# Layer 0's routing: the engine that clears the table of shares

## The chip, the cores and the metric

The kernel runs on one core of a Trainium2 chip. A core has five engines, each with its own queue of instructions, which it takes strictly in order: TensorE (PE; its weight loads are listed apart as PEld), VectorE (DVE), ScalarE (ACT), GpSimd (POOL) and SyncE (SP, which here only starts transfers). They wait for each other through semaphores. The metric is the device time of one execution in microseconds (us); lower is better.

## The reference

A stack of four layers on 4 rows of 512 tokens with 128 channels, float32. Each layer adds half a feed-forward part, then attention, then half the same feed-forward part again, always on a normalized copy of `x`. The change lies in the feed-forward part of layer 0, a mixture of eight experts of which each token uses two, and a ninth, shared expert:

```
x = x + 0.5 * _L0_ffn_ref(_layernorm(x), ...)
x = x + _L0_attn_ref(_layernorm(x), ...)
x = x + 0.5 * _L0_ffn_ref(_layernorm(x), ...)
...
def _L0_ffn_ref(x, gate_w, gate_b, w1, b1, w3, b3, w2, b2, sw1, ...):
    scores = softmax(xt @ gate_w.T)
    _, idx = top_k(scores + gate_b, 2)
    weights = take_along_axis(scores, idx)
    comb = (weights[..., None] * one_hot(idx, 8)).sum(1)
    for each expert:  acc += comb[:, e] * (swiglu((xt @ w1 + b1) * (xt @ w3 + b3)) @ w2 + b2)
    shared = swiglu((xt @ sw1 + sb1) * (xt @ sw3 + sb3)) @ sw2 + sb2
    return acc + shared
```

`comb` is the table of shares: per token, the weight of each of the eight experts, zero for those not chosen.

## The kernel before

The kernel is one long program. Its first stage, some 90 us, is the routing of layer 0's first feed-forward part (`by_expert`, `route`). `route(b)` handles one of the four rows, its 512 tokens as 4 tiles of 128: normalize (`layernorm_parts`; the power step L322 is on GpSimd), transpose (L342), gate matmul (L517), exponentials and the ranking of the experts on VectorE (L365 to L370, `taken` L528, `sofar` L533), two small matmuls that count tokens ahead of each other (L540, L541), the destination rows `irows` (L544 to L549), and then eight indirect transfers from GpSimd's queue (L586) that scatter the row's tokens into `sorted_x`, expert by expert.

Beside it the table `comb` is made: a tile of 128 partitions by 4 x 32 floats, of which columns 0 to 7 are the experts' shares and column 8 is 0.5 for the shared expert; the rest has to be zero, since the whole tile is transposed by TensorE (L568) and multiplied with the experts' biases (L573, added to `x` by L353). L551 clears it, `weigh` writes column 8 (L554) and the shares (L555), then computes `share` (L557 to L560). `comb` comes from a pool with two buffers, so the clear for row b+2 has to wait until row b's table has been transposed (L568) and read (L557).

While the rows are routed, TensorE and the others do two more things: `fold` (L635, L636) subtracts weights from each other, 16 matmuls of 128x512, and `common` (L606 to L626) computes the shared expert for every row: L606 fills one of three `big` accumulator tiles with two matmuls, ScalarE takes one half (L608), VectorE the other (L611), so that the tile comes free. `plan` (L646 to L698) then turns the counts into a list of tiles, `iwho`. From about 90 us on, `tiles` fetches sorted tiles (`xs`, L740, on SyncE's queue; each fetch waits for all 32 scatters), transposes them (L751) and runs the experts (L761 and after).

Then comes layer 0's attention (`l0_attn_quick`, scores L1203, values L1217, the reciprocal of the sums L1229, its use L1237 and L1239, output L1246). There TensorE's order is written out by hand, and in its gaps rows 0 to 2 are routed a second time, for the second feed-forward part; so `route` runs eight times in all, and L551 with it.

Except for TensorE in attention and a last stretch that has an order of its own, the order in each engine's queue is not that of the source: a scheduler puts each engine's instructions in an order it thinks they can run in. Moving one instruction to another engine therefore also changes the order of others around it.

The file also holds a second, safer version of the whole program behind a condition; it does not run with these inputs.

Of the kernel before, what the change touches and what calls it, by code (L numbers as in the profile page):

```python
# [270 lines left out]
def program(ctx: ExitStack, tc: tile.TileContext, a: dict, out: bass.AP, worst):  # L271

    nc = tc.nc
# [191 lines left out]
    def by_expert(w, rooms, key):  # L465
# [33 lines left out]
        def route(b, work, rows_pool=None, slow=False):  # L499
# [48 lines left out]
            nc.vector.tensor_reduce(rows[:, b], mine, AX.X, ALU.add)  # L548
            nc.vector.tensor_copy(irows[:, b], rows[:, b])  # L549
            comb = tiny.tile([P, NT, 32], F32, tag="comb", name="comb", bufs=2)  # L550
            nc.gpsimd.memset(comb, 0.0)  # L551

            def weigh():
                nc.vector.memset(comb[:, :, NE], 0.5)  # L554
# [405 lines left out]
        def fetched(b, work):  # L960
# [19 lines left out]
            while got:  # L980
                yield DVE(0.35, at=got[0][3])
                add()

        return SimpleNamespace(route=route, common=common, fold=fold, plan=plan, tiles=tiles, back=back, ready=ready, fetched=fetched, tiled=tiled, needs=needs)

    def chain(*parts):
# [1841 lines left out]
```

## Time and profile before

| | us |
|---|---|
| median of three runs | 1305.28 |
| the three runs | 1305.28, 1298.9, 1309.57 |
| the profiled execution | 1288.94 |
| its span, first to last instruction | 1287.2 |
| L551, the eight clears: one takes | 0.204 to 0.236 |
| starts of the first and last of them | 0.7, 450.8 |
| VectorE waiting at L554 for L551, 3 times | 12.0 in all |
| an indirect transfer L586 on GpSimd, 64 of them | 1.108 mean |

In the profile a line of the timeline has the start, the length, the engine, the source line, the operation, what it writes and reads with shapes, how many records were merged, and in brackets how long the engine stood idle before it and what ended that. A float32 matmul appears as two records. "issue" is idle time in which the engine waited for nothing that the profile shows. A chain of waits is followed back from the last instruction: at each step to what released it. The granted clock is the share of its full clock that TensorE was given.

### The profile page before, as it was taken

Reading aid. Unit: us, or ns where it says so; the run is one execution under the profiler, and the core shown is the slowest. Engines: PE = TensorE matmul, PEld = TensorE weight load, DVE = VectorE, ACT = ScalarE, POOL = GpSimd, SP = SyncE. Lnnn points to the kernel's source line nnn. Section 1 sums busy time; section 2 is a strip of 40 time slices with the busy share of each in tenths; the row PEclk is TensorE's granted clock in tenths of the full one; section 3 lists DMA queues with packets and bytes.
Section 4 is the critical chain, followed back from the end, with each engine's and each line's share of the span. In section 5 each row is a group of like instructions: output and inputs, shape, how many; then the busy total and the mean of one; then the engine's idle time right before and its main releaser. Section 6 shows DMA issues by size and latency. Waiting matters only on the chain.

```text
span 1287.2 us, 20162 instructions
## 1 busy us (share of the span) xinstructions
PE 1174.3 (91%) x6954; PEld 630.3 (49%) x6954; DVE 895.4 (70%) x2328; ACT 700.6 (54%) x1015; POOL 328.1 (25%) x320
## 2 busy tenths in 40 slices
PE   5899989999999999988899949989999999999995
PEld 3455644334335335355455548765596544543333
DVE  5597767888988988769667945868735873365233
ACT  2435535653644544533345523556757777787872
POOL 4340223032220400202123554533224121041000
PEclk9899989999999999989899987899999999999998
DMA  8123311121110210201321140000011000000000
GB/s 308 33 73 90 89 60 52 66 76 38 57 66 33 80 48 37 67 1 40 106 73 44 36 133 23 26 12 23 26 50 38 5 18 18 17 25 1 9 9 11
DMA packets 63490, 65.00 MB, mean 50 GB/s; under 512 B 11538, under 2 KB 53908, under 8 KB 62868
## 3 DMA queue, kind: packets, MB, share of 16 engines
q1 hardware_dynamic: 57236, 51.04, 11.9%
q0 software_dynamic: 6144, 12.60, 3.3%
q8 instruction: 58, 0.95, 0.3%
q14 instruction: 52, 0.42, 0.1%
HBM read 29.13 MB, written 17.69 MB: 36 GB/s over the span
## 4 chain that ended last, share of the span: by engine, by line
PE 63%; DVE 21%; issue 5%; DMA 3%; ACT 3%; POOL 2%; SPq 1%; DVEq 0%; POOLq 0%; ACTq 0%
PE big L1956 8%; PE one L1998 8%; PE big L1203 5%; PE one L1217 5%; PE big L761 4%; PE one L1541 3%; PE big L883 3%; PE one L1246 2%; PE big L606 2%; DVE sums L1212 2%; PE big L1153 2%; PE one L2475 1%; PE one L2019 1%; PE big L635 1%; PE one L794 1%
## 5 line engine op out<-in xcount | busy, mean ns | idle before, releaser
L1972 ACT ACTIVATE pT<-big 128x1024 f32<-128x1024 f32 (+1 forms) x224 | 205.0, 963 | 52.7 <-PE big L1956 44.3
L1204 ACT ACTIVATE pT<-big 128x1024 f32<-128x1024 f32 x128 | 125.7, 1034 | 55.7 <-PE big L1203 53.0
L1203 PE MATMUL big<-qk 64*128 64x512 f32 x512 | 127.5, 609 | 6.8 <-DVE U L1239 6.8
L1956 PE MATMUL big<-qkq,qkk 32*128 32x512 f32 (+3 forms) x1024 | 130.9, 555 | 0.1
L1217 PE MATMUL one<-pT,V 128*64 128x512 f32 x512 | 116.9, 598 | 0.0
L1998 PE MATMUL one<-pT,V 128*32 128x512 f32 (+3 forms) x1024 | 111.5, 522 | 2.5 <-DVE through L2029 0.8
L1504 POOL TENSOR_TENSOR rs<-rs,root 128x4 f32<-128x4 f32 x35 | 37.1, 1059 | 226.8 <-DVE rs L1502 183.5
L586 POOL DMA_INDIRECT sorted_x<-xn,irows x64 | 70.9, 1108 | 69.8 <-DVE share L558 22.4
L1212 DVE TENSOR_TENSOR sums<-sums,pT 128x1024 f32<-128x1024 f32 x64 | 78.1, 1220 | 5.7 <-ACT pT L1204 1.1
L1203 PEld LDWEIGHTS big<-qk 64*128 64x128 f32 x512 | 46.6, 187 | 69.5 <-issue 40.9
L1956 PEld LDWEIGHTS big<-qkq,qkk 32*128 32x128 f32 x1024 | 49.2, 184 | 61.8 <-issue 40.8
L883 PE MATMUL big<-w_w,xsT 128*128 x156 | 76.2, 620 | 2.5 <-ACT xsT L1355 2.4
L761 PE MATMUL big<-w_w,xsT 128*128 x156 | 73.5, 595 | 0.4 <-issue 0.4
L1217 PEld LDWEIGHTS one<-pT,V 128*64 128x64 f32 x512 | 33.9, 136 | 77.1 <-issue 72.4
L842 POOL DMA_INDIRECT yg<-sorted_y,ito x32 | 40.1, 1254 | 123.0 <-DMA sorted_y<-ys 61.8
L1294 ACT COPY U<-one 128x512 f32<-128x512 f32 x32 | 18.8, 587 | 94.7 <-PE one L1217 92.6
L606 PE MATMUL big<-xnT,w_w 128*128 128x512 f32 x128 | 61.4, 616 | 6.9 <-DVE u L611 5.8
L353 DVE TENSOR_TENSOR x<-x,one 128x512 f32<-128x512 f32 x31 | 21.2, 684 | 57.2 <-PE one L1541 33.1
L1984 DVE TENSOR_TENSOR pT<-pT,w_c_tri 128x256 f32<-128x256 f32 (+1 forms) x96 | 52.4, 563 | 2.5 <-ACT pT L1972 2.2
L608 ACT ACTIVATE t<-big,w_bs 128x512 f32<-128x512 f32 x32 | 21.7, 685 | 56.5 <-PE big L606 30.9
L322 POOL TENSOR_TENSOR rs<-rs,root 128x4 f32<-128x4 f32 x16 | 20.7, 1298 | 118.7 <-DVE rs L321 118.6
L1998 PEld LDWEIGHTS one<-pT,V 128*32 128x32 f32 x1024 | 23.9, 108 | 54.6 <-issue 37.9
(448 smaller groups left out, 2418.4 us busy)
## 6 DMA issues: line engine op xcount, KB each, us to landing
other<-qk SPq DMA_DIRECT2D x64, 256.0 KB, 2.2
xs<-sorted_x SPq DMA_DIRECT2D x78, 64.0 KB, 1.8
sorted_y<-ys SPq DMA_DIRECT2D x38, 128.0 KB, 1.8
w_w<-in_w SPq DMA_DIRECT2D x2, 2048.0 KB
w_l_w<-in_l_w SPq DMA_DIRECT2D x8, 256.0 KB, 3.2
w_l_w<-in_l_w SPq DMA_DIRECT2D x1, 2048.0 KB, 8.4
X<-row_x SPq DMA_DIRECT2D x8, 256.0 KB, 3.5
row_y<-y SPq DMA_DIRECT2D x8, 256.0 KB, 2.3
```

The lines of the kernel that those rows point to most:

```text
L586: apart(nc.gpsimd.indirect_dma_start(out=sorted_x[:, :], out_offset=bass.IndirectOffsetOnAxis(ap=irows[:, b, j, t : t + 1], axis=0), in_=x ...
L606: nc.tensor.matmul(pa[:, m, :], lhsT=w["w13"][:, NE, m, odd, c * P : (c + 1) * P], rhs=xTs[b], start=True, stop=True)
L761: nc.tensor.matmul(pa[:, k, :], lhsT=st[u]["xT"][:, k * P : (k + 1) * P], rhs=w["w13"][:, bass.ds(st[u]["e"][k], 1), m].rearrange("p o a b ...
L883: nc.tensor.matmul(pa[:, k, :], lhsT=xT[:, k * P : (k + 1) * P], rhs=w["w13"][:, bass.ds(e[k], 1), m].rearrange("p o a b -> p (o a b)"), s ...
L1203: nc.tensor.matmul(sT[:, u, :], lhsT=k[r, t * P : (t + 1) * P], rhs=q[r, :], start=True, stop=True)
L1204: nc.scalar.activation(pT[:, :, t % 2, :], sT, AF.Exp, scale=scale)
L1212: nc.vector.tensor_tensor(s, s, pT[:, :, m, :], ALU.add)
L1217: nc.tensor.matmul(po[r, :], lhsT=V[:, t, :], rhs=pT[:, u, t % 2, :], start=(t == 0), stop=(t == NT - 1), tile_position=(0, 64 * u))
L1956: nc.tensor.matmul(sT[j // 2][:, j % 2, c : c + n], lhsT=keys[k][r, t * P : (t + 1) * P], rhs=turns[k, g][r, S - n :], start=True, stop=True)
L1972: nc.scalar.activation(p[:, :, :n], sets[i][h][:, :, :n], AF.Exp, scale=scale)
L1984: nc.vector.tensor_tensor(d, d, w["c_tri"].unsqueeze(1).unsqueeze(1).to_broadcast([P, 2, len(parts), P]), ALU.min)
L1998: nc.tensor.matmul(po[32 * j : 32 * j + 32, S - n :], lhsT=V[k % 2][:, t, NJ * g + j, :], rhs=us[i][j // 2][:, j % 2, c : c + n], start=(t ...
```

## The change

L551 is issued on VectorE instead of GpSimd. Nothing else is edited.

```diff
@@ -548,7 +548,7 @@
             nc.vector.tensor_reduce(rows[:, b], mine, AX.X, ALU.add)
             nc.vector.tensor_copy(irows[:, b], rows[:, b])
             comb = tiny.tile([P, NT, 32], F32, tag="comb", name="comb", bufs=2)
-            nc.gpsimd.memset(comb, 0.0)
+            nc.vector.memset(comb, 0.0)
 
             def weigh():
                 nc.vector.memset(comb[:, :, NE], 0.5)
```

In the order that the scheduler makes of it, the eight clears are gone from GpSimd's queue. On VectorE two stand at the very start, two right behind `share` of rows 0 and 1 (L558), two beside the first tiles, and one each behind the routing of rows 0 and 1 in attention, directly ahead of L554. In the first 90 us the order of other instructions shifts too: one more matmul of `fold` stands ahead of row 0's L573, the first L606 pair ahead of row 2's gate matmul, and VectorE's steps of `route`, `common` and `plan` are interleaved differently. In attention VectorE's steps of normalization (L331) and of `irows` change places by one or two, and before the first tile fetch SyncE starts one more zero-fill of `row_y` (L2706). After about 455 us the order is the same.

## The prediction

> **What bounds the kernel now.** I read the page first, for who is on the path that sets the end.
>
> ```profile
> span 1287.2 us, 20162 instructions
> PE 1174.3 (91%) x6954; PEld 630.3 (49%) x6954; DVE 895.4 (70%) x2328; ACT 700.6 (54%) x1015; POOL 328.1 (25%) x320
> PE 63%; DVE 21%; issue 5%; DMA 3%; ACT 3%; POOL 2%; SPq 1%; DVEq 0%; POOLq 0%; ACTq 0%
> ```
>
> TensorE (PE) is busy nine tenths of the span, so only what makes TensorE wait, or slows it, can pay. The eight clears of `comb` (L551) are 8 x 0.23 = 1.9 us of GpSimd (POOL), which is idle for three quarters of the time: their work is worth nothing. What can be worth something is who waits for them. The list of waits of `comb` names one pair: VectorE (DVE) at L554 waited for the clear three times, 12.0 us in all. So I went to the chain that ended last, in the first 100 us (columns: start, length, piece):
>
> ```profile
> 43.86 6.22 issue
> 50.09 0.06 DVE comb L554
> 50.97 3.78 PE big L606 x4
> ```
>
> The longest of these waits, 6.2 us, is on the chain itself. The timelines of the three engines there say why:
>
> ```profile
> 43.44 0.42 DVE L366 TENSOR_TENSOR eq<-biased 128x256 f32<-128x256 f32 x1
> 50.09 0.06 DVE L554 MEMSET comb<- 128x4 f32 x1 [6.24 <-POOL comb L551]
> 50.16 0.75 DVE L611 SCALAR_TENSOR_TENSOR u<-big,w_bs,t 128x512 f32<-128x512 f32 x1
> 48.83 0.97 POOL L586 DMA_INDIRECT sorted_x<-xn,irows  x1 [0.30 <-issue]
> 49.79 0.23 POOL L551 MEMSET comb<- 128x128 f32 x1
> 40.91 5.31 PE L606 MATMUL big<-xnT,w_w 128*128 128x512 f32 x12
> 50.97 3.78 PE L606 MATMUL big<-xnT,w_w 128*128 128x512 f32 x4 [4.74 <-DVE u L611]
> ```
>
> The clear takes 0.23 us, but it stands in GpSimd's queue behind the eight scatters of row 1 (L586, the first at 39.25). VectorE's small memset L554 needs it, and VectorE keeps its order, so L611 behind it waits too. L611 empties the first `big` bank; there are three, TensorE has filled them all by 46.2 and stands 4.74 us. What follows is in the busy time by stretch (columns: length, then busy time of PE, PEld, DVE, ACT, POOL, then the granted clock):
>
> ```profile
> 46.00:51.00 5.00, 0.26 (x2) 0.04 (x1) 0.90 (x3) 0.53 (x1) 3.13 (x4) 0.83 0.15 52
> 51.00:56.00 5.00, 5.00 (x11) 2.94 (x12) 5.00 (x18) 1.94 (x4) 0.02 (x1) 0.50 0.01 3
> 50.00:60.00 10.00, 9.04 (x28) 5.34 (x29) 8.31 (x33) 4.59 (x8) 0.16 (x3) 0.69 0.03 8
> 60.00:70.00 10.00, 9.61 (x25) 4.16 (x24) 9.73 (x30) 6.60 (x11) 7.87 (x8) 1.00 0.14 48
> 70.00:80.00 10.00, 8.91 (x35) 4.85 (x34) 9.57 (x36) 2.97 (x5) 6.33 (x8) 1.00 0.29 87
> 80.00:90.00 10.00, 9.31 (x50) 5.67 (x49) 9.24 (x22) 3.68 (x6) 2.97 (x5) 1.00 0.24 70
> ```
>
> After the pause TensorE gets half its clock for 5 us (0.50), so it loses another 5.0 x 0.5 = 2.5 us. And from 50 to 90 VectorE is full (36.9 of 40 us): there it sets the pace as much as TensorE.
>
> The other two waits:
>
> ```profile
> 30.99 0.16 DVE L533 TENSOR_TENSOR sofar<-sofar,taken 128x8 f32<-128x8 f32 x1 [4.77 <-issue]
> 365.27 0.23 POOL L551 MEMSET comb<- 128x128 f32 x1
> 365.57 0.06 DVE L554 MEMSET comb<- 128x4 f32 x1 [4.58 <-POOL comb L551]
> 383.28 1.14 PE L1237 MATMUL big<-rsum,w_c_spread 32*128 32x512 f32 x8 [1.66 <-DVE rsum L1229]
> 471.85 1.14 PE L1237 MATMUL big<-rsum,w_c_spread 32*128 32x512 f32 x8 [0.71 <-DVE rsum L1229]
> ```
>
> The first is row 0's clear at 30.71, labelled "issue" because in the program L554 stands just ahead of L533; TensorE folds weights (L635) from 21.7 to 34.9 without a break, so it is hidden. The second is in layer 0's attention, 4.58 us. TensorE has work of its own there until row 1 ends, where it waits 1.66 us for `rsum`; at row 2's end, where the wait for the clear was only 1.13 us, it waits 0.71.
>
> **The change part by part.**
>
> *Removed: eight clears from GpSimd.* Their 1.9 us are covered by idle time there; no scatter or power step that the path waits for moves up by more than 0.24 us. I take 0.
>
> *Removed: the 6.24 us wait at 44.* If TensorE alone counted, 4.74 + 2.5 = 7.2 us come back; if the clock were slow for another reason, 4.7. What VectorE can give is its idle time, 6.24, and it is full afterwards. I followed the new program's order by hand with the row durations. One more fold matmul (0.86, the chain's piece at 38.46) now precedes L573, so row 1's `irows` come at about 39.2 instead of 38.15, and its scatters, 10.6 us, end at about 50.9. The first L606 pair stands before row 2's gate and ends near 40.8; L608 (0.69) and L611 follow, so the first bank is free at 42.8, before TensorE asks for it at 46. VectorE then runs without a gap: row 2's `irows` near 52.7 (59.04 before), row 3's near 65.9 (72.03), `iwho` near 76.6 (83.48). All three move up by 6.1 to 6.9. Row 3's scatters move with them, so the fetch of the first tiles (86.27) does too. A new wait of about 1.8 us appears on TensorE ahead of row 3's L540; it is inside these numbers. Taken: 6.2, nearest to VectorE's own idle row; ends 4.7 and 7.2.
>
> *Removed: the 4.58 us wait at 361.* Next late there is `rsum`, which also needs L1223's result; so the gain is what row 1 waits more than row 2, 1.66 - 0.71 = 0.95. Ends: 0, and 1.66. The waits at 30 and at 450 (1.13) give 0: fold and row 2's 0.71 remain.
>
> *Added: eight clears on VectorE.* The trace has no VectorE memset of that size. Below lies the 128x12 memset (0.07, L251), above it the lone 128x128 tensor_scalar (0.34, L331); GpSimd's 0.23 lies between, and I take 0.2. By the new order two run before the first input lands (2.55 us idle), two right after `share` of rows 0 and 1, where VectorE next waits for the gate matmul anyway (1.54 and 1.24 us idle), two beside the first tiles, where TensorE is full for 58 of 58 us. Only the two in attention are uncovered, 2 x 0.2 = 0.4 us; at row 2 the wait of 1.13 us that goes pays for its clear, so 0.2 remains. Ends 0 and 8 x 0.34 = 2.7 with no cover at all.
>
> *Added: waits.* Four clears in the new order wait for TensorE's transpose L568 themselves. Behind them stand the gate's maximum (L386) or the rotation (L1164). L568 stands ahead of that gate matmul in TensorE's queue, so L386 could not run sooner; in attention L568 ends at 360.84 and 450.36, and VectorE comes free at 361.0 and 449.99, where it waits today as well. Cost 0, at most the 0.37 us of the second.
>
> *Moved: DMAs.* One zero-fill of `row_y` (0.42 us on SyncE's queue) now comes before the first tile fetch, not after. It runs while the last scatters land (83.2 to 86.27): 0.
>
> Sum: 6.2 + 0.95 - 0.2 = 7.0 us, so 1288.94 - 7.0 = 1281.9 for the profiled execution (1287.2 span and 1.7 around it). It was 16 us faster than the median of the three runs, 1305.28, which themselves span 10.7 us. I carry the difference: 1305.28 - 7.0 = 1298.
>
> The row to hold against this is VectorE's 9.73 and 9.57 of 10 us. The Trainium skill (Perfetto Trace Analysis, Optimizing Scalar/DVE Operations) advises giving a saturated VectorE's work away, even to GpSimd, and warns that the two share a port so that exchanges may not help. By it the change gains nothing and adds its clears, up to 2.7 us. The rows speak otherwise because the price was a place in a queue. For the half clock, TensorE: Matmul & The Clock Gate (The HAM clock gate) gives a window of 3.4 us, an estimate of 1.7 us lost after the pause; the row has 2.5. With 1.7, TensorE's part would be 6.4, still above what I took.
>
> **The rivals.**
>
> *It goes as summed:* 1298; 0.74.
>
> *The gain is lost at the next gate.* If the tiles cannot start earlier, only 0.95 - 0.2 stays: about 1304.5. For: the first fetch waits for all 32 scatters, and GpSimd needs 10.6 us per row. Against: the chain at 84 to 94 runs over L624, L611 and L619, not over the fetch, and the scatters are themselves released by `irows`. 0.12.
>
> *Slower: VectorE comes late for TensorE at row 3's L540.* The new order puts L611, L618 and L619 of the shared expert among row 3's ranking. I have TensorE there at 60.0 and `taken` at 61.8. A pause of the size that halved the clock before costs its length w plus 2.5, and w is over 4.5 before it eats the 7.0. That needs 2.7 us more VectorE work than counted. With w = 8 it is 3.5 us slower: 1309. For: VectorE is full there. Against: the same work fits today. 0.09.
>
> *More:* both ends high, 7.2 + 1.66, gives 8.9: 1296.4. 0.05. That the change does nothing is excluded: the new order has all eight on VectorE.
>
> **How the numbers follow.** A median of three of runs that spread 10.7 us is uncertain by some 5 either way, and 1% (13 us) is about what a measurement of this kernel tells from no change. From 1296 to 1309 by the cases; with that uncertainty, most of it below where most of the chance lies, 1288 to 1310. Faster by over 1% means below 1292.2: the main case with 6 us of luck, 0.16. Slower by over 1% means above 1318.3: the slower rival with bad luck, 0.06. Within: 0.78.
>
> **What would show it.** No wait of VectorE for GpSimd at L554; TensorE without the 4.74 us pause near 46 and with a clock near 1.00 from 50 to 60; first tile transposes (L751) at about 83 instead of 89.66; `rsum` wait of row 1 near 0.7; L551 on VectorE at about 0.2 us. A new pause above 3 us on TensorE before 90, or L751 still near 89, would prove me wrong.

## The result, and the profile after

The changed kernel took 1293.49 us (median of 22 runs) where the kernel before took 1298.7 (22 runs on the same chip): 0.9967 of it, 95% interval 0.9949 to 0.9984, so 4.3 us less (2.1 to 6.6). The ratio is not the quotient of the two medians, which lie 5.2 us apart; the gains named below go by the ratio. Beside the experiments the change was timed twice more, on two other chips, where the kernel before took 1280.47 and 1282.73: 0.9979 [0.995, 1.0007] and 0.9975 [0.995, 0.9999]. The mean of the three is some 3.4 us, 0.26%, about half of the 7.0 us of the sum. The forecast's 1298 stood on the first three runs of the kernel before, 1305.28; with 22 runs that median is 1298.7, so the time was lower than forecast though the gain was smaller. That 1293.49 lies between 1288 and 1310 says little for the mechanism: the range was that wide for the base of three runs, and the base fell by 6.6 us.

The page of the changed kernel; its execution took 1293.41 us, which is more than the 1288.94 of the one before:

```profile
span 1291.5 us, 20152 instructions
PE 1170.9 (91%) x6954; PEld 624.4 (48%) x6954; DVE 896.4 (69%) x2336; ACT 700.3 (54%) x1015; POOL 329.2 (25%) x312
PE 66%; DVE 16%; issue 6%; POOL 3%; DMA 3%; ACT 2%; SPq 1%; another core or an unknown queue 0%; POOLq 0%; DVEq 0%; ACTq 0%
```

VectorE's share of the chain fell from 21% to 16%. The span says nothing about the change: the part from the first L883 to the last L1956, from about 615 us on, where the order is the same in both, took 640.0 us before and 647.0 in this execution; in two others of the changed kernel it took 632.8 and 633.6. So the profiles are read by where a line starts, counted from the first transpose (L342).

The view of the tile `comb` has all eight clears (duration in ns, least, median and most):

```profile
L551 DVE MEMSET comb<- x8: 165/165/165, 0.9 to 448.5; 128x128 f32 x8
```

and the timeline of VectorE has the clear and its reader in the first pass and in attention:

```profile
39.70 0.17 DVE L551 MEMSET comb<- 128x128 f32 x1
39.94 0.06 DVE L554 MEMSET comb<- 128x4 f32 x1
360.24 0.17 DVE L551 MEMSET comb<- 128x128 f32 x1
360.48 0.06 DVE L554 MEMSET comb<- 128x4 f32 x1
```

A clear takes 0.165 us, and no wait is put down to it any more. On TensorE the 4.74 us pause is gone, but others stand further on (timeline of TensorE; the last figure in brackets is who ended the wait):

```profile
54.85 5.42 PE L606 MATMUL big<-xnT,w_w 128*128 128x512 f32 x12 [0.66 <-DVE u L611]
61.89 0.39 PE L540 MATMUL one<-taken,w_c_before 128*128 128x40 f32 x2 [1.62 <-DVE sofar L531]
64.02 1.91 PE L606 MATMUL big<-xnT,w_w 128*128 128x512 f32 x2
84.80 0.46 PE L624 MATMUL one<-w_w,h 128*128 128x128 f32 x2 [0.61 <-DVE h L619]
85.36 0.30 PE L751 MATMUL one<-w_c_ident,xs 128*128 128x128 f32 x1
85.97 0.33 PE L751 MATMUL one<-w_c_ident,xs 128*128 128x128 f32 x1 [0.31 <-DMA xs<-sorted_x]
86.90 0.30 PE L751 MATMUL one<-w_c_ident,xs 128*128 128x128 f32 x1 [0.61 <-DMA xs<-sorted_x]
87.67 0.44 PE L751 MATMUL one<-w_c_ident,xs 128*128 128x128 f32 x1 [0.47 <-DMA xs<-sorted_x]
88.37 3.35 PE L761 MATMUL big<-w_w,xsT 128*128 x4 [0.26 <-issue]
```

Two new pauses: 1.62 us ahead of row 3's L540, and 1.4 us in three pieces for the fetched tiles. After each of them matmuls take twice as long: a pair of L606 takes 1.91 (1.12 in other profiles), the four records of the first L761 take 3.35 (1.98). The busy time by stretch has the clock (last three columns: granted clock, DMA share, GB/s):

```profile
46.00:51.00 5.00, 5.00 (x20) 2.60 (x18) 4.85 (x21) 3.98 (x7) 4.09 (x4) 1.00 0.12 39
50.00:60.00 10.00, 9.34 (x31) 4.43 (x29) 8.93 (x29) 7.43 (x12) 6.72 (x7) 1.00 0.12 40
60.00:70.00 10.00, 7.97 (x30) 5.12 (x30) 8.18 (x33) 2.05 (x5) 4.72 (x5) 0.83 0.15 47
84.00:88.00 4.00, 1.90 (x7) 0.86 (x6) 3.68 (x13) 1.58 (x3) 0.00 (x0) 0.97 0.30 83
88.00:92.00 4.00, 3.74 (x9) 1.85 (x9) 2.62 (x25) 0.61 (x2) 0.00 (x0) 0.60 0.28 75
```

From 46 to 51 TensorE is now full at clock 1.00, where before it was busy 0.26 us; so the first pause went as forecast. But the clock loss came back twice: 10 x 0.17 = 1.7 us at 60 to 70, and 4 x 0.4 = 1.6 us at 88 to 92. Where the second comes from is in the chain of waits:

```profile
78.15 1.50 POOL sorted_x L586
79.66 0.23 POOL zeros L2702
...
83.32 0.36 SPq L740
...
85.84 1.79 DMA xs<-sorted_x
87.63 0.04 issue
87.67 0.44 PE one L751
```

The chain now runs from row 3's scatters over GpSimd's queue, the zero-fills and the fetches into L751. Before, the first fetch started at 86.27, and TensorE, coming to L751 at 89.66, waited for none of the first four tiles (its one wait there is for a copy on ScalarE):

```profile
86.27 9.58 SPq L740 DMA_DIRECT2D xs<-sorted_x  x12
89.66 0.38 PE L751 MATMUL one<-w_c_ident,xs 128*128 128x128 f32 x2
90.51 0.59 PE L751 MATMUL one<-w_c_ident,xs 128*128 128x128 f32 x2 [0.46 <-ACT xsT L754]
```

It now comes at 85.36, ahead of three of the first four.

In attention the wait for `rsum` at the end of row 1 fell from 1.66 us to that of row 2:

```profile
381.60 1.14 PE L1237 MATMUL big<-rsum,w_c_spread 32*128 32x512 f32 x8 [0.71 <-DVE rsum L1229]
```

### The profile page after: what moved, and what is told of

It is laid out like the page before. It is cut to its first block, busy times and chain, and to the rows that moved or that the text cites. A ratio compares the mean times of both kernels' runs of the same rounds, so it can differ in the third digit from the quotient of the medians.

```text
span 1291.5 us, 20152 instructions
## 1 busy us (share of the span) xinstructions
PE 1170.9 (91%) x6954; PEld 624.4 (48%) x6954; DVE 896.4 (69%) x2336; ACT 700.3 (54%) x1015; POOL 329.2 (25%) x312
## 4 chain that ended last, share of the span: by engine, by line
PE 66%; DVE 16%; issue 6%; POOL 3%; DMA 3%; ACT 2%; SPq 1%; another core or an unknown queue 0%; POOLq 0%; DVEq 0%; ACTq 0%
PE big L1956 9%; PE one L1998 8%; PE big L1203 7%; PE one L1217 7%; PE big L761 3%; PE one L1541 3%; PE big L883 2%; PE one L1246 2%; PE big L606 2%; PE big L1153 2%; PE one L2475 1%; PE one L2019 1%; PE big L635 1%; DVE sums L1212 1%; PE one L794 1%
## 5 line engine op out<-in xcount | busy, mean ns | idle before, releaser
L1956 PE MATMUL big<-qkq,qkk 32*128 32x512 f32 (+3 forms) x1024 | 133.2, 565 | 3.6 <-ACT pT L1972 3.4
L586 POOL DMA_INDIRECT sorted_x<-xn,irows x64 | 73.5, 1149 | 68.7 <-issue 22.6
L1956 PEld LDWEIGHTS big<-qkq,qkk 32*128 32x128 f32 x1024 | 50.1, 187 | 65.7 <-issue 42.9
L883 PE MATMUL big<-w_w,xsT 128*128 x156 | 75.4, 613 | 2.4 <-ACT xsT L1355 2.0
L761 PE MATMUL big<-w_w,xsT 128*128 x156 | 74.8, 604 | 0.3 <-issue 0.3
L1217 PEld LDWEIGHTS one<-pT,V 128*64 128x64 f32 x512 | 33.9, 136 | 77.1 <-issue 72.9
L353 DVE TENSOR_TENSOR x<-x,one 128x512 f32<-128x512 f32 x31 | 21.2, 683 | 64.0 <-PE one L1541 34.3
L606 PE MATMUL big<-xnT,w_w 128*128 128x512 f32 x128 | 60.0, 604 | 1.7 <-DVE u L611 1.7
L1209 DVE TENSOR_TENSOR sums<-pT 128x1024 f32<-128x1024 f32 x32 | 39.1, 1221 | 18.8 <-PE one L1223 10.0
## 6 DMA issues: line engine op xcount, KB each, us to landing
other<-qk SPq DMA_DIRECT2D x64, 256.0 KB
w_l_w<-in_l_w SPq DMA_DIRECT2D x8, 256.0 KB
X<-row_x SPq DMA_DIRECT2D x8, 256.0 KB
row_y<-y SPq DMA_DIRECT2D x8, 256.0 KB
```

What stands on the lines that cost most here:

```text
L586: apart(nc.gpsimd.indirect_dma_start(out=sorted_x[:, :], out_offset=bass.IndirectOffsetOnAxis(ap=irows[:, b, j, t : t + 1], axis=0), in_=x ...
L606: nc.tensor.matmul(pa[:, m, :], lhsT=w["w13"][:, NE, m, odd, c * P : (c + 1) * P], rhs=xTs[b], start=True, stop=True)
L761: nc.tensor.matmul(pa[:, k, :], lhsT=st[u]["xT"][:, k * P : (k + 1) * P], rhs=w["w13"][:, bass.ds(st[u]["e"][k], 1), m].rearrange("p o a b ...
L883: nc.tensor.matmul(pa[:, k, :], lhsT=xT[:, k * P : (k + 1) * P], rhs=w["w13"][:, bass.ds(e[k], 1), m].rearrange("p o a b -> p (o a b)"), s ...
L1217: nc.tensor.matmul(po[r, :], lhsT=V[:, t, :], rhs=pT[:, u, t % 2, :], start=(t == 0), stop=(t == NT - 1), tile_position=(0, 64 * u))
L1956: nc.tensor.matmul(sT[j // 2][:, j % 2, c : c + n], lhsT=keys[k][r, t * P : (t + 1) * P], rhs=turns[k, g][r, S - n :], start=True, stop=True)
```

## The experiments

Two theories stood at the start. Mine: the clear's place in GpSimd's queue was the price, in two places that add, and the first pass gives part of its gain back at new pauses. The rival: the gain comes from attention alone, and the first pass gives nothing in the end. Times are against the kernel before on the same chip: 1280.7 us (34 runs) beside e1, e2, e3 and e5, 1280.47 (35) beside a2, e4, e6 and f1, 1282.73 (29) beside a3, k2, e5 again and f2.

Stages by the profiles, one execution each, in us: the first L751, counted from the first L342; the tile stage, first to last L761; the clock at 88 to 92; attention's stage, first to last L1246; and the first L883, again from L342, where the first feed-forward part and attention are over. They come from starts printed to 0.1 us, so each is good to about 0.1.

| kernel | ratio, interval | L751 | tile stage | clock 88-92 | attention | L883 |
|---|---|---|---|---|---|---|
| before | | 80.3 | 110.8 | 1.00 | 256.1 | 606.8 |
| the change | 0.9967 [0.9949, 0.9984] | 76.5 | 112.4 | 0.60 | 254.9 | 605.1 |
| a2, the change | 0.9979 [0.995, 1.0007] | 75.8 | 113.5 | 0.50 | 254.8 | 603.7 |
| a3, the change | 0.9975 [0.995, 0.9999] | 75.6 | 113.5 | 0.50 | 254.9 | 603.3 |
| e1 | 0.9958 [0.993, 0.9987] | 75.1 | 109.0 | 1.00 | 255.9 | 599.1 |
| e2 | 0.9985 [0.9956, 1.0013] | 81.0 | 111.1 | 1.00 | 254.7 | 604.5 |
| e3 | 0.9948 [0.9918, 0.9978] | 73.7 | 109.6 | 1.00 | 256.0 | 598.2 |
| e5 | 0.993 [0.9905, 0.9955] | 73.6 | 109.5 | 1.00 | 255.0 | 597.6 |
| e5 again | 0.9931 [0.99, 0.9961] | 72.9 | 110.8 | 1.00 | 254.6 | 596.8 |
| e4 | 0.9995 [0.9963, 1.0026] | 75.9 | 113.8 | 0.50 | 254.8 | 604.4 |
| e6 | 0.9988 [0.9961, 1.0016] | 75.9 | 113.7 | 0.50 | 254.7 | 603.8 |
| f1 | 0.9982 [0.9951, 1.0012] | 75.4 | 110.7 | 1.00 | 255.3 | 602.7 |
| k2 | 0.9956 [0.9931, 0.9981] | 76.2 | 110.7 | 1.00 | 254.7 | 600.5 |
| f2 | 0.9922 [0.9889, 0.9954] | 70.9 | 109.9 | 1.00 | 255.0 | 595.6 |

**e1 and e2: each half of the change alone.** `key` is 1 in the first pass and 2 in the second.

```diff
-            nc.gpsimd.memset(comb, 0.0)
+            (nc.vector if key == 1 else nc.gpsimd).memset(comb, 0.0)   # e1; key == 2 in e2
```

> Only the four clears of the first pass of routing go to VectorE; the four of the second pass stay on GpSimd. If the gain comes from the first pass (the 6.2 us wait at 44 us gone, part of it given back before the tiles): no pause of TensorE near 46 us, first expert matmul (L761) near 88 us as in the changed kernel instead of 91.5, the 4.58 us wait of VectorE at 361 us still there with 1.66 us of TensorE's wait for rsum behind it, and the time 2 to 4 us below the kernel before. If all that the first pass gains is given back and only attention gains: the time of the kernel before, within 1 us.

> Only the four clears of the second pass go to VectorE. Both theories want the 6.2 us wait at 44 us unchanged and the wait at 361 us gone, with TensorE's wait for rsum at 0.71 instead of 1.66 us. First-pass theory: about 1 us faster than the kernel before (ratio 0.999). Attention theory: the whole 4 to 5 us of the changed kernel (ratio 0.9967).

e1 took 1276.64 us, 5.4 less than before (1.7 to 9.0), more than the 2 to 4 expected; e2 1278.7, 1.9 less, not told from zero. Together that is 7.3, where the whole change gave 2.7 to 4.3; the intervals are too wide to call this a difference, but e1's profile kept the clock at the first tiles, which all three profiles of the change lost. Their profiles divide as meant. In e1 VectorE still waits for the clear in attention:

```profile
358.15 0.06 DVE L554 MEMSET comb<- 128x4 f32 x1 [4.58 <-POOL comb L551]
```

and in e2 TensorE still makes the old pause in the first pass:

```profile
51.27 3.78 PE L606 MATMUL big<-xnT,w_w 128*128 128x512 f32 x4 [4.74 <-DVE u L611]
```

Attention's stage takes 256.1, 255.9 and 256.0 us in the three kernels that clear on GpSimd there, and 254.6 to 255.3 in the eleven profiles with VectorE: 1.1 us between the means. The rival falls: the first pass alone gives a gain that is told from zero.

**e3, e5: the clears stay on GpSimd in the first pass, but four tables take the wait away.** e5 clears on VectorE in the second pass.

```diff
-    def by_expert(w, rooms, key):
+    def by_expert(w, rooms, key, combs=None):
...
-            comb = tiny.tile([P, NT, 32], F32, tag="comb", name="comb", bufs=2)
-            nc.gpsimd.memset(comb, 0.0)
+            comb = (combs or tiny).tile([P, NT, 32], F32, tag="comb", name="comb", bufs=4 if combs else 2)
+            (nc.vector if key == 2 else nc.gpsimd).memset(comb, 0.0)   # e5; nc.gpsimd in e3
...
-        mix = by_expert(w0, rooms, 1)
+        mix = by_expert(w0, rooms, 1, work)
```

> All clears stay on GpSimd, but the first pass has four tables instead of two, so its four clears run at the start and nothing waits for them. If the gain is the place in GpSimd's queue and not the engine: no wait of VectorE at L554 before 90 us, no pause of TensorE near 46 us, and a gain like that of the first pass alone, 2 to 6 us. If a clear on VectorE itself were what helps: the time of the kernel before.

> Four tables for the first pass on GpSimd, and the second pass's clears on VectorE: no wait for a clear is left anywhere. If the two places add up: the gain of the run with four tables plus about 1 us, so 3 to 7 us below the kernel before and no slower than the changed kernel. If the first pass's gain is set by the scatters of row 3 in any case: the changed kernel's time.

> e5 once more, on GpSimd with four tables in the first pass and on VectorE in the second: 0.993 of before [0.9905, 0.9955] the first time, 9.0 us less. If that is its own size, it is 7 to 10 us faster than before again, and 4 to 6 faster than the changed kernel beside it; if the first was luck, its gain is that of the changed kernel, 2.6 to 4.3. In its profile the first pass should again have no pause ahead of L540 and a clock of 1.00 through 40 to 90.

e3 took 1274.51 us, 6.7 less than before (2.8 to 10.5), with every clear on GpSimd, and VectorE's waits for the clear in the first pass are gone (0.2 us left): what counts is when the clear is over, not which engine does it. The scheduler gave e3 and e5 another order in the first pass, on TensorE and the other engines too, so their size is not that of the wait alone. e5 gave 9.0 and 8.9 less (0.993 and 0.9931), more than the 3 to 7 first expected, and stood at 1273.8 beside the changed kernel's 1278.5: it beats both. In its second profile the first pass keeps the full clock; TensorE has three short waits and none ahead of L540:

```profile
57.96 1.12 PE L606 MATMUL big<-xnT,w_w 128*128 128x512 f32 x2 [1.03 <-DVE u L611]
60.48 1.13 PE L606 MATMUL big<-xnT,w_w 128*128 128x512 f32 x2 [0.20 <-DVE u L611]
67.83 2.41 PE L606 MATMUL big<-xnT,w_w 128*128 128x512 f32 x5 [0.78 <-DVE u L611]
```

```profile
50.00:60.00 10.00, 8.97 (x22) 3.74 (x22) 9.19 (x35) 6.47 (x9) 6.88 (x7) 1.00 0.11 38
60.00:70.00 10.00, 9.02 (x35) 4.88 (x34) 9.78 (x37) 3.56 (x7) 6.21 (x7) 1.00 0.29 88
80.00:90.00 10.00, 8.80 (x36) 4.80 (x36) 9.99 (x55) 3.22 (x6) 0.00 (x0) 1.00 0.27 74
```

Its first L751 stands at 72.9 to 73.6 after L342. My forecast for the change, 83 with L342 at 9.4, is 73.6. So the 6.2 us are there to be had, though by another order than the one the forecast followed; the changed kernel does not reach them.

**e4: four tables, cleared on VectorE in both passes.** It is e5 with `nc.vector.memset(comb, 0.0)` throughout. TensorE, ScalarE, GpSimd and SyncE then have the changed kernel's order.

> Four tables in the first pass, as in e3, but cleared by VectorE, in both passes. TensorE, ScalarE, GpSimd and SyncE keep the changed kernel's order; e3 had another order on TensorE and no pause ahead of row 3's L540. Theory (what counts is only when a clear is over, not who does it, and the rest of the gain hangs on TensorE's order): it is like the changed kernel, within 1 us, with the 1.6 us wait ahead of L540 near 60, and about 2 us slower than e5 (0.993 of before), which differs from it in e3's order. Rival (the clears on VectorE between the routing's steps are what holds the changed kernel back): without them there it is as fast as e5, 9.0 us faster than before, and the wait ahead of L540 is gone.

It took 1279.78 us, 0.9995 of before: like the changed kernel within the intervals, not like e5. The pauses of the changed kernel are there, and the half clock behind them (3.78 in place of 1.98):

```profile
61.77 0.39 PE L540 MATMUL one<-taken,w_c_before 128*128 128x40 f32 x2 [1.62 <-DVE sofar L531]
88.16 3.78 PE L761 MATMUL big<-w_w,xsT 128*128 x4 [0.22 <-issue]
```

So the clears among the routing's steps are not what holds the changed kernel back. Its four other queues have the order that the scheduler made when the clears went to VectorE, and with it come the pauses. VectorE's own order shows one reason: between row 2's L353 and row 3's `taken` (L528) the changed kernel has ten steps of the shared expert (L611 to L619), and that stretch takes 8.2 us; e5 has seven, and 6.7 us. No run moved these steps alone.

**e6: every clear twice.**

```diff
-            nc.vector.memset(comb, 0.0)
+            nc.vector.memset(comb, 0.0); nc.vector.memset(comb, 0.0)
```

> The changed kernel with every clear of the table done twice on VectorE, sixteen in place of eight; nothing else moves but a few VectorE steps beside them. By the profile of the changed kernel a clear takes 0.165 us, 1.3 us for eight. If the clears lie under cover as I counted (only the two in attention uncovered), it costs 0.2 to 0.4 us against the changed kernel, not to be told from zero; if VectorE's time in the routing is itself the path, the first pass's four and attention's four cost all of 1.3 us or, with a longer pause at L540 and a longer half clock, 2 to 4.

1278.93 us against 1277.84 for the changed kernel beside it; the first L751 stands at 75.9 against 75.8, the first L883 at 603.8 against 603.7. Eight more clears cost nothing that can be told, so by the stages they lie under cover.

**f1: the zero-fills behind the first fetches.** Of the changed kernel's queues only SyncE's differs. f2 is e5 with the same edit.

```diff
+   got_in.append(got)     # behind each fetch, L740
...
-                nc.sync.dma_start(out=px[e * P : (e + 1) * P, :], in_=zeros)
+                tc.add_manual_dep(nc.sync.dma_start(out=px[e * P : (e + 1) * P, :], in_=zeros).ins, got_in[9].name, mybir.DependencyInfo(mybir.DependencyClass.NoSync, ...), ...)
```

(and the same for `row_y`, L2706).

> The changed kernel with the zero-fills of row_x and row_y (L2705, L2706) placed on SyncE behind the first fetches of tiles; the other engines' order is the same. In the changed kernel four of them ran between the last scatter and the first fetch, which began 5.17 us after the last scatter's start (4.02 before), and TensorE waited 1.4 us for fetched tiles, then had half its clock for 3.4 us. Theory (the fills are part of what the change gave back): first fetch 1 to 2 us earlier after the last scatter, L751's waits for the fetch under 0.5 us in all, and 1 to 3 us faster than the changed kernel. Rival (the scatters landing are the gate, the fills run in their shadow): the fetch begins at the same distance from the last scatter, and the time is the same within 0.5 us.

> e5 with the zero-fills of row_x and row_y behind the first fetches, as in f1. In e5's profile TensorE still waited for the first tiles for under 1.2 us, at full clock, so there is little left to gain: theory, L761 begins 0.3 to 1 us earlier than in e5, and the time is that of e5 within 1 us. Rival (the fills' traffic later in the tile stage, where they now stand beside the stores and later fetches, delays those): tile stage longer by over 1 us and the time 1 to 3 us above e5.

In the changed kernel the last scatter ends at 78.15 + 1.50 = 79.65 and the first fetch starts at 83.32, 3.67 later (3.68 in a2, 3.38 in a3); before it was 86.27 - 83.22 = 3.05. In f1 (GpSimd's and SyncE's queues):

```profile
77.70 1.50 POOL L586 DMA_INDIRECT sorted_x<-xn,irows  x1 [0.30 <-issue]
82.32 9.57 SPq L740 DMA_DIRECT2D xs<-sorted_x  x12
```

that is 3.12. So by these profiles the fills cost some 0.3 to 0.55 us there, not the 1 to 2 I expected; the 3.12 that are left pass with no fill in between. (Before, with three fills, it was 3.05, so the figure is hardly above the spread. From e5 to f2 it went from 3.38 to 2.26.) TensorE still waited 1.13 us for the fetches, where I expected under 0.5, and the time, 0.9982, cannot be told from the changed kernel's. f2 is like e5 (1274.68 against 1273.8). It stood 2 us earlier at L751, but its row 3 was already that much earlier at L540 (48.1 after L342 against 50.0), ahead of the fetches, so this is not the fills' work; its tile stage of 109.9 speaks against the rival.

**a2 and a3: the change again. k2: TensorE kept busy while it waits for the first tiles.** k2 adds eight transposes of the identity ahead of the first two pairs of tiles, overwritten by the true ones.

```diff
             def turn(u):
-                px = one()
+                px = one(); [nc.tensor.transpose(px[:, j * P : (j + 1) * P], ident, ident) for j in range(2) for _ in range(2) if u < 2]
```

> The changed kernel once more, beside its own variants. On the other chip it took 0.9967 of the kernel before [0.9949, 0.9984], 4.3 us less; e1 and e2, each half of it, gave 5.4 and 1.9 less, 7.3 together. If the halves simply add, it is 7.3 us faster than before (0.9943); if its own size on the other chip holds, 4.3 (0.9967). In the profile, if the shortfall of the first pass is a rule and not an accident of one execution: TensorE waits about 1.6 us ahead of row 3's L540 near 60 us and its clock drops to about half within 60 to 68, and TensorE waits for the fetched tiles at L751 for about 1.4 us in all. If it was an accident, the clock is near 1.00 there.

> The changed kernel a third time, beside the three below. So far 0.9967 [0.9949, 0.9984] and 0.9979 [0.995, 1.0007]: 2.6 to 4.3 us less than before; I expect the same again. Both of its profiles, and those of e4 and e6, had half the clock for about 3.4 to 6 us at the first tiles (87 to 93 us), and their tile stage (first to last L761) took 112.4 to 113.8 us; e1 and f1 have the same order on TensorE there and pauses of nearly the same size, kept a clock of 1.00, and took 109.0 and 110.7. Theory (the clock there is decided anew in each execution, by pauses just at the limit): either is possible here, and the tile stage is about 3 us longer with the half clock than without.

> The changed kernel with eight transposes of the identity added on TensorE, four ahead of each of the first two pairs of tiles (L749; their results are overwritten by the true transposes); the order is otherwise the same but for seven L624 one place earlier. They fill part of the 1.9 to 2.2 us that TensorE stood idle from 84 to 88 us, and cost at most 8 x 0.3 = 2.4 us. Theory (the pauses for the fetched tiles take the clock, and that is what the change gives back there): clock 1.00 from 84 to 94, tile stage near 110 in place of 112 to 114, and 1 to 3 us faster than the changed kernel. Rival (the half clock is not set off by those pauses): it comes all the same, and the time is the same or up to 2.4 us more.

a2 gave 2.7 us less and a3 3.2, nearer the change's own 4.3 than the 7.3 of the two halves together; both have the 1.62 us wait ahead of L540 and the half clock at both places. a3 and k2 at 84 to 92 us, each from the windows of its own profile, first a3:

```profile
84.00:88.00 4.00, 1.95 (x7) 1.00 (x7) 3.68 (x14) 1.89 (x4) 0.00 (x0) 0.80 0.28 77
88.00:92.00 4.00, 4.00 (x7) 1.93 (x8) 2.40 (x24) 0.37 (x2) 0.00 (x0) 0.50 0.30 81
```

then k2:

```profile
84.00:88.00 4.00, 2.72 (x16) 1.60 (x14) 3.68 (x13) 1.58 (x3) 0.00 (x0) 1.00 0.28 78
88.00:92.00 4.00, 3.63 (x20) 2.52 (x20) 3.76 (x28) 0.37 (x1) 0.00 (x0) 1.00 0.27 74
```

With 2.72 us of work in 84 to 88 in place of 1.95 the clock stayed at 1.00, and the first L883 came at 600.5 in place of 603.3. The time was 0.9956 against a3's 0.9975, 1.5 us by the medians, with intervals that overlap: the profile shows the direction, the times do not prove it. Nor does one profile prove that the added work held the clock, for e1 had the changed kernel's pauses there and kept the clock too:

```profile
84.00:88.00 4.00, 2.03 (x7) 1.07 (x8) 3.68 (x18) 1.91 (x4) 0.00 (x0) 1.00 0.29 83
88.00:92.00 4.00, 4.00 (x21) 2.70 (x20) 2.92 (x25) 1.01 (x1) 0.00 (x0) 1.00 0.27 72
```

e1 and the change have the same order here on TensorE, and a2, with 2.12 us of work in that stretch, lost the clock.

A finer reading of the same traces tells them apart. The half clock begins and ends on a grid of 3.41 us: in the changed kernel it holds from 63.87 to 67.28 and from 87.76 to 91.17, seven steps later. So TensorE's work is counted here within one such step. a3's step at the first tiles, with the one after it:

```profile
82.99:86.40 3.41, 1.87 (x8) 0.67 (x7) 2.95 (x9) 1.58 (x3) 0.00 (x0) 1.00 0.23 65
86.40:89.81 3.41, 2.85 (x5) 1.23 (x6) 3.41 (x26) 0.37 (x1) 0.00 (x0) 0.50 0.30 82
```

and e1's:

```profile
82.47:85.88 3.41, 1.99 (x9) 0.76 (x7) 2.82 (x8) 1.58 (x3) 0.00 (x0) 1.00 0.22 63
85.88:89.29 3.41, 2.42 (x6) 1.14 (x7) 3.41 (x26) 0.37 (x1) 0.00 (x0) 1.00 0.27 77
```

In a3 most of the pauses fall into one step, 1.54 us idle; in e1 the grid cuts them into 1.42 and 0.99; in k2 the added work leaves 1.08. From 30 to 100 us, over all fourteen profiles, the step ahead of a half clock was idle for 1.54 us or more (15 of 15), and no step that kept the full clock for more than 1.49 (f1). This was read afterwards, and no run tested it. Nor is idle time alone the rule further on: e4 kept its clock after a step with 1.88 us idle, from 162.27, and a2 lost it after one with 0.4, from 864.46.

What can also be told is the price: the tile stage took 112.4 to 113.8 us in the five profiles with the half clock, 109.0 to 111.1 in the nine without. In what share of executions it comes was not tried.

## Why the forecast held in direction and was too high

*The 6.24 us wait at 44, taken at 6.2.* This is the term that was mis-sized. The wait and the pause went as forecast, and the new order ran as followed by hand at first: row 2's `irows` at 52.52 (52.7 forecast), TensorE ready for L540 at 60.27 (60.0), `taken` at 61.57 (61.8), a wait of 1.62 (1.8). The step that failed is what the prediction says of this new wait: "it is inside these numbers". Its length was, the half clock after it was not: I had counted lost clock only for a "pause of the size that halved the clock before", 4.74 us, and 1.62 us was enough, for 1.7 us. Row 3's `irows` then came at 67.32 (65.9) and the first L751 at 85.36, not 83: 3.8 us earlier than before, counted from L342, where 6.7 was forecast (4.5 and 4.7 in a2 and a3). e5, whose order has no such pause, reached the 73.6 forecast. With VectorE taking 8.2 us over that stretch, ten steps of the shared expert among the ranking, this is the place that the slower rival named.

*The rival at the next gate, 0.12.* It was priced as all or nothing, and it happened in part. Not weighed was how little slack the fetch had: it began at 86.27, and TensorE came for its tiles at 89.66. Counted from L342, TensorE came 3.8 us earlier and the fetch only 2.5; TensorE waited 1.4 us, and in three of three profiles lost the clock after it. So of the 6.7 us forecast some 2 to 3 were lost by the first L751, and most of the rest at the tiles: by the last L761 the changed kernel was only 0.5 to 1.0 us ahead (191.9, 192.4 and 192.1 after L342, against 192.9).

*The slower rival.* Its place was right, its price rule was not: it too counted clock loss only from a pause like that of 4.74 us.

*Attention, 0.95 less 0.2 for the clears.* The wait for `rsum` fell by just 0.95, and the stage became 1.2 us shorter. e2 alone gave 1.9 us, which its interval, 5.6 less to 1.7 more, cannot pin down.

*The clears, 0.2 in all.* 0.165 us each; e6 shows no price for doubling them. *The zero-fill, 0:* 0.3 to 0.55 us of the fetch's delay for all four fills, by f1, hardly above the spread. *The wait at 30, 0:* not tried by itself.

On the clock, the Trainium skill (TensorE: Matmul & The Clock Gate, The HAM clock gate) has one idle window of about 3.4 us as what halves it, and windows that run on their own, so that the same kernel meets them at different places. The rows differ in the first: 1.62 us with a few short gaps beside it, 1.75 to 2.03 us idle out of a step of 3.41, halved the clock in all eight profiles that have it. They fit the second: the same order at nearly the same pauses lost the clock at the first tiles in five profiles and kept it in e1 and f1.

## What to carry to other kernels

A cheap instruction is worth its place in its queue: find what stands ahead of it and who waits behind its reader, and then either move it or make it ready earlier with another buffer, which here gave more, with the order that the scheduler then made; nobody planned that order, so look at it anew after each such move. When a long pause of TensorE goes, look for the two or three gates behind it whose slack is smaller than the gain, and price a pause of even 1.6 us with the half clock that can follow it. A change of a few microseconds is not seen in one execution's span; it is seen in where the stages start.

## What the runs showed of the hardware

- A pause of 1.62 us on TensorE was followed by half its clock for some 3.4 us in eight of eight profiles (0.83 over 60 to 70 us); waits of some 1.03, 0.20 and 0.78 us, spread over 10 us, were not, in four of four.
- Pauses of 1.8 to 2.2 us in sum out of 4 us lost the clock in some profiles and not in others. The half clock began and ended on a grid of 3.41 us; between 30 and 100 us it followed each step with 1.54 us idle or more (15 of 15) and none with 1.49 or less, but later in the program idle time alone did not decide it.
- A memset of 128x128 float32 took 0.165 us on VectorE and 0.204 to 0.245 on GpSimd.
- Most scatters took some 0.97 us of GpSimd's time, single ones in the first 90 us up to 1.63; the last of row 3 was 0.97 in one profile of the changed kernel and 1.50 in two others.
